# Causal attention of one stage: a hand-written order over both batches, the mask as a bf16 product, copies on ScalarE

## The chip, the cores and the metric

The kernel runs on one core of one Trainium2 chip. The time is device microseconds of one execution; lower is better. Three runs of the kernel before gave 4184.93, 4197.97 and 4197.70 us, with the median 4197.7 us. A fourth execution was profiled, and all durations below are from it.

## The reference

The kernel computes a network of eight layers on an input of 2 batches, 1024 positions and 128 features in fp32. Every layer is added to the running state `x`, after a normalisation of `x` over the features. The third layer, a causal attention with one head, is the one that the change touches:

```python
def _layernorm(x, axis=-1, eps=1e-05):
    m = jnp.mean(x, axis=axis, keepdims=True)
    v = jnp.var(x, axis=axis, keepdims=True)
    return (x - m) / jnp.sqrt(v + eps)

def _L0_attn_b_ref(x, wqk, wov):
    b, n, d = x.shape
    mask = jnp.triu(jnp.full((n, n), -jnp.inf, dtype=x.dtype), k=1)
    q = jnp.einsum('bnd,de->bne', x, wqk)
    scores = jnp.einsum('bne,bme->bnm', q, x) + mask
    attn = jax.nn.softmax(scores, axis=-1)
    ctx = jnp.einsum('bnm,bmd->bnd', attn, x)
    return jnp.einsum('bnd,de->bne', ctx, wov)
...
x = x + _L0_ffn_ref(_layernorm(x, axis=-1), ...)
x = x + _L0_attn_b_ref(_layernorm(x, axis=-1), L0_attn_b_wqk, L0_attn_b_wov)
x = x + _L0_ffn_ref(_layernorm(x, axis=-1), ...)
```

## The kernel before

The state lies in SBUF, features on the 128 partitions, in four tiles `xt[0]` to `xt[3]` of 512 positions; `xt[0]` and `xt[1]` are batch 0. The stages run one after another: the windowed attention `attn_a0`, the experts `ffn0`, the causal attention `attn_b0`, `ffn0` again, `attn_a1`, then the six deep layers (`Layers`) and the rest. In `attn_a0`, `ffn0` and `Layers` the order of the work on each engine is the order in which the program names it (`manual_schedule` with the engines of `ORDERED`). In `attn_b0` a scheduler puts the order together.

`attn_b0` (L237 to L290) first does, for each of the four blocks of 512 positions, a normalisation (`self.norm`): four transposes on TensorE (PE) at L120 so that positions lie on the partitions, statistics on VectorE (DVE; L124, L125), the inverse root on ScalarE (ACT; L134) and a reciprocal (L135), the scaling on DVE (L143), four transposes back (L152) and a copy to `xn` on ACT (L155). Then come the projection `pq` (L253) with its copy to `qT` on ACT (L254), and the product of the block with `wov`, `pw` (L257), with its copy to `xw` on DVE (L258). ACT reaches the square root and the exponential through different function tables, and a change of table is an instruction of its own in the profile (ACT_TABLE_LOAD).

The second loop goes over the batches and over eight blocks `i` of 128 query positions. For a block it computes the scores against all keys up to its own (L265; one or two products of up to 512 columns into a PSUM tile `sc`), adds the causal mask to the last 128 columns on DVE (L268), takes the negative maximum (L270), the exponential with its sum on ACT (L273) into `pr`, and the reciprocal of the sum (L274). Then the probabilities are transposed in groups of up to four blocks of keys (L163, called through `to_psum`), copied from PSUM to `pT` on DVE (L280) and multiplied with `xw` into `y` (L282). The result is divided by the sum on DVE (L286), transposed back (L288) and added to `xt` on DVE (L290). PSUM holds two banks for transposes and projections (tag `tp`), two score tiles of two banks each (`sc`) and one bank for `y`.

An fp32 product appears in the profile as two matmul instructions, a transpose as one.

Of the kernel before, what the change touches and what calls it, by code (L numbers as in the profile page):

```python
# [10 lines left out]
F32 = mybir.dt.float32  # L11
BF16 = mybir.dt.bfloat16
AF = mybir.ActivationFunctionType
ALU = mybir.AluOpType
AX = mybir.AxisListType
PSUM = bass.MemoryType.PSUM

P = 128
B, N, D = 2, 1024, 128
T = B * N  # L20
NBLK = T // 512
EPS = 1e-5
# [19 lines left out]
ORDERED = {  # L42
    mybir.EngineType.PE, mybir.EngineType.Activation, mybir.EngineType.DVE, mybir.EngineType.Pool,
}


class Net:
# [186 lines left out]

    def attn_b0(self, key):  # L237
        nc, tc = self.nc, self.tc
        with ExitStack() as ctx:
            cp = ctx.enter_context(tc.tile_pool(name="b0c", bufs=1))  # L240
            sb = ctx.enter_context(tc.tile_pool(name="b0s", bufs=2))
            ps = ctx.enter_context(tc.tile_pool(name="b0ps", bufs=2, space=PSUM))
            wqk, wov = self.w["b0"][:, 0:D], self.w["b0"][:, D : 2 * D]
            causal = self.w["b0_mask"]
            xn = [cp.tile([P, N], F32, tag=f"xn{b}", name=f"b0xn{b}") for b in range(B)]
            qT = [cp.tile([P, N], F32, tag=f"q{b}", name=f"b0q{b}") for b in range(B)]
            xw = [cp.tile([P, N // P, D], F32, tag=f"xw{b}", name=f"b0xw{b}") for b in range(B)]
            for b in range(B):
                for k in range(2):
                    x = xn[b][:, ts(k, 512)]  # L250
                    self.norm(self.xt[2 * b + k], x, ps, f"{key}_{b}_{k}")
                    pq = ps.tile([P, 512], F32, tag="tp", name=f"b0pq{b}{k}")
                    nc.tensor.matmul(pq, wqk, x, start=True, stop=True)  # L253
                    nc.scalar.copy(qT[b][:, ts(k, 512)], pq)  # L254
                    pw = ps.tile([P, 4, D], F32, tag="tp", name=f"b0pw{b}{k}")
                    for c in range(4):
                        nc.tensor.matmul(pw[:, c, :], x[:, ts(c, P)], wov, start=True, stop=True)  # L257
                    nc.vector.tensor_copy(xw[b][:, ts(k, 4), :], pw)  # L258
            for b in range(B):
                for i in range(N // P):  # L260
                    n = P * (i + 1)
                    sc = ps.tile([P, N], F32, tag="sc", name=f"b0sc{b}{i}")
                    for c in range(0, n, 512):
                        m = min(512, n - c)
                        nc.tensor.matmul(  # L265
                            sc[:, ds(c, m)], qT[b][:, ts(i, P)], xn[b][:, ds(c, m)], start=True, stop=True
                        )
                    nc.vector.tensor_tensor(sc[:, ts(i, P)], sc[:, ts(i, P)], causal, ALU.add)  # L268
                    mx = self.small.tile([P, 1], F32, tag="bmx", name=f"b0mx{b}{i}")
                    nc.vector.tensor_reduce(mx, sc[:, 0:n], AX.X, ALU.max, negate=True)  # L270
                    pr = sb.tile([P, N], F32, tag="pr", name=f"b0pr{b}{i}")
                    sm = self.small.tile([P, 1], F32, tag="bsm", name=f"b0sm{b}{i}")
                    nc.scalar.activation(pr[:, 0:n], sc[:, 0:n], AF.Exp, bias=mx, accum_out=sm)  # L273
                    nc.vector.reciprocal(sm, sm)  # L274
                    y = ps.tile([P, D], F32, tag="y", name=f"b0y{b}{i}", bufs=1)
                    for c in range(0, i + 1, 4):
                        m = min(4, i + 1 - c)
                        tp = self.to_psum(ps, "tp", lambda j: pr[:, ts(c + j, P)], f"b0tp{b}{i}{c}", m)
                        pT = sb.tile([P, 4, P], F32, tag="pT", name=f"b0pT{b}{i}{c}", bufs=3)
                        nc.vector.tensor_copy(pT[:, 0:m, :], tp[:, 0:m, :])  # L280
                        for j in range(m):
                            nc.tensor.matmul(  # L282
                                y, pT[:, j, :], xw[b][:, c + j, :], start=(c + j == 0), stop=(c + j == i)
                            )
                    o = sb.tile([P, D], F32, tag="o", name=f"b0o{b}{i}")
                    nc.vector.tensor_scalar(o, y, sm, None, ALU.mult)  # L286
                    tp = ps.tile([P, 4, P], F32, tag="tp", name=f"b0to{b}{i}")
                    nc.tensor.transpose(tp[:, 0, :], o, self.ident)  # L288
                    x = self.xt[2 * b + i // 4][:, ts(i % 4, P)]
                    nc.vector.tensor_tensor(x, tp[:, 0, :], x, ALU.add)  # L290

# [284 lines left out]
class Experts:  # L578
# [19 lines left out]
    def bank(self, tag, name):  # L598
        bufs = {"b": 4, "x3": 2, "h": 1, "x2": 1}[tag]
        return self.ps.tile([P, 512], F32, tag=tag, name=f"f0{name}_{self.key}", bufs=bufs)  # L600
# [863 lines left out]
```

## Time and profile before

| | |
|---|---|
| median of three runs | 4197.7 us (4184.93 to 4197.97) |
| profiled execution | 4190.64 us |
| its span, first to last instruction | 4188.8 us |
| mean granted clock of TensorE | 0.958 |
| PE, DVE, ACT, POOL busy, share of the span | 94%, 74%, 57%, 59% |
| `attn_b0`: first transposes (L120) to those of the next stage | 391.92 to 486.58 us |

The profile's page gives the busy time of each engine over the span, and cuts the span into 40 slices of 104.7 us in which each digit is a busy share in tenths. In its row PEclk the digit is the clock that TensorE was granted, in tenths of full speed. The busy time by stretch gives the same for any window. A timeline row has the start and the length in us, the engine, the line, the operation, the tiles written and read with their shapes, and in brackets how long the engine had been idle and whose work ended that. PEld are the weight loads of TensorE, which overlap its products. POOL is GpSimd.

### The profile page before, as it was taken

The numbers are of one execution on the slowest core, as the hardware profiler recorded it, in microseconds if no ns is written. First come the engines' busy times: TensorE is split into PE (matmuls) and PEld (weight loads), VectorE is DVE, ScalarE is ACT, GpSimd is POOL, SyncE is SP. The second block draws the span as 40 slices with busy tenths as digits, with TensorE's granted clock in tenths as the row PEclk, the third lists the DMA queues.
The fourth block names the chain that finished last, engine by engine and source line by source line (L and its number), as shares of the span: only waits on it lengthen the run. The fifth ranks groups of instructions, "written<-read, shape, count | busy, mean of one in ns | idle before, by whom it ended". The sixth has DMA issues, their size and how long they took to land.

```text
span 4188.8 us, 156424 instructions
## 1 busy us (share of the span) xinstructions
PE 3932.2 (94%) x67608; PEld 2556.2 (61%) x67608; DVE 3107.2 (74%) x5983; ACT 2401.4 (57%) x4507; POOL 2457.2 (59%) x1578
## 2 busy tenths in 40 slices
PE   7789796899999999999999848999999999999998
PEld 4543533566666666666666525666666666666665
DVE  6843545778878787878878657787887878787886
ACT  3433232676666666666666416766666666666665
POOL 1322022777677776776766217776766777667762
PEclk8789898999999999999999968999999999999999
DMA  1000001223233332232222103232233322323222
GB/s 56 2 1 1 1 0 32 81 71 84 74 76 84 76 85 72 73 90 71 69 66 68 45 16 91 73 84 74 74 84 76 84 73 72 91 68 77 62 67 56
DMA packets 181572, 261.53 MB, mean 62 GB/s; under 512 B 51100, under 2 KB 74264, under 8 KB 180632
## 3 DMA queue, kind: packets, MB, share of 16 engines
q1 hardware_dynamic: 180888, 251.52, 23.4%
q8 instruction: 538, 8.81, 0.9%
q14 instruction: 146, 1.20, 0.1%
HBM read 52.09 MB, written 1.05 MB: 13 GB/s over the span
## 4 chain that ended last, share of the span: by engine, by line
PE 82%; DVE 3%; ACT 1%; POOL 1%; issue 1%; DMA 0%; SPq 0%; ACTq 0%; DVEq 0%; POOLq 0%
PE pj_l L943 16%; PE y_l L1174 9%; PE pv_l L1045 9%; PE tqk_l L163 9%; PE av_l L1142 8%; PE sc_l L1092 6%; PE tpr_l L163 4%; PE to_l L163 4%; PE fg_l L1248 3%; PE fy_l L1284 3%; PE fa_l L1269 3%; PE sc_l L1083 2%; PE f0x_e L760 1%; PE f0h_e L693 1%; PE f0x_e L693 1%
## 5 line engine op out<-in xcount | busy, mean ns | idle before, releaser
L972 DVE TENSOR_TENSOR t_l<-pj_l,rot_l 128x512 f32<-128x512 f32 x1536 | 967.9, 684 | 370.3 <-ACT sq_l L952 357.4
L989 POOL TENSOR_TENSOR raw_l<-t_l,t_l 128x1024 f32<-128x1024 f32 x384 | 908.4, 2366 | 530.2 <-DVE on_l L1150 336.2
L943 PE MATMUL pj_l<-wqkv_l,x_l 128*128 128x512 f32 x1536 | 783.3, 612 | 8.1 <-DVE t_l L972 5.7
L1004 POOL TENSOR_TENSOR raw_l<-raw_l,rn_l 128x1024 f32<-128x1024 f32 x384 | 723.1, 1901 | 95.3 <-ACT rn_l L999 88.3
L952 ACT ACTIVATE sq_l<-pj_l 128x512 f32<-128x512 f32 x768 | 461.7, 603 | 369.4 <-PE pj_l L943 361.4
L978 POOL TENSOR_TENSOR sq_l<-sq_l 128x512 f32<-128x512 f32 x384 | 490.9, 1278 | 310.3 <-ACT sq_l L952 307.1
L163 PE MATMUL tqk_l<-ident_sb,raw_l 128*128 128x128 f32 x3072 | 453.2, 279 | 17.0 <-POOL raw_l L1004 14.7
L163 PEld LDWEIGHTS tqk_l<-ident_sb,raw_l 128*128 128x128 f32 x3072 | 356.9, 142 | 162.4 <-issue 123.4
L1022 ACT COPY qT_l<-tqk_l 128x512 f32<-128x512 f32 x384 | 224.8, 585 | 387.6 <-PE tqk_l L163 387.6
L1045 PE MATMUL pv_l<-wqkv_l,x_l 128*128 128x512 f32 x768 | 415.6, 623 | 5.8 <-DVE ln_xn_fl L1228 5.3
L1174 PE MATMUL y_l<-outT_l,wo_l 128*128 128x128 f32 x3072 | 393.7, 281 | 0.0
L1092 PEld LDWEIGHTS sc_l<-kT_l,qT_l 64*32 64x32 f32 x24576 | 294.9, 105 | 155.0 <-issue 144.4
L1174 PEld LDWEIGHTS y_l<-outT_l,wo_l 128*128 128x128 f32 x3072 | 357.5, 191 | 18.2 <-issue 1.0
L1142 PE MATMUL av_l<-vw_l,pT_l 64*32 64x64 f32 x24576 | 358.9, 224 | 3.7 <-issue 3.6
L943 PEld LDWEIGHTS pj_l<-wqkv_l,x_l 128*128 128x128 f32 x1536 | 255.0, 192 | 171.9 <-issue 106.6
L1054 ACT COPY v_l<-pv_l 128x512 f32<-128x512 f32 x384 | 225.0, 586 | 223.0 <-PE pv_l L1045 202.9
L1142 PEld LDWEIGHTS av_l<-vw_l,pT_l 64*32 64x32 f32 x24576 | 292.9, 105 | 71.9 <-issue 65.7
L1150 DVE TENSOR_TENSOR on_l<-av_l,inv_l 128x512 f32<-128x512 f32 x384 | 247.5, 686 | 120.0 <-PE av_l L1142 119.8
L1092 PE MATMUL sc_l<-kT_l,qT_l 64*32 64x64 f32 x24576 | 329.2, 223 | 0.0
L163 PEld LDWEIGHTS tpr_l<-ident_sb,pr_l 128*128 128x128 f32 x1536 | 188.9, 141 | 152.1 <-issue 116.2
L1102 DVE TENSOR_TENSOR pr_l<-sc_l,mx_l 128x512 f32<-128x512 f32 x384 | 265.6, 692 | 13.2
L1101 DVE TENSOR_REDUCE mx_l<-sc_l 128x8 f32<-128x512 f32 x384 | 261.4, 681 | 3.4 <-PE sc_l L1092 3.4
(344 smaller groups left out, 6158.1 us busy)
## 6 DMA issues: line engine op xcount, KB each, us to landing
vw_l<-v_l SPq DMA_DIRECT2D x3024, 64.0 KB
wqkv_l<-in_Wqkv SPq DMA_DIRECT2D x36, 512.0 KB
rot_l<-in_rotary SPq DMA_DIRECT2D x24, 512.0 KB
wo_l<-in_Wo SPq DMA_DIRECT2D x12, 512.0 KB
w_l<-in_W SPq DMA_DIRECT2D x12, 341.0 KB
f_sb<-in_f SPq DMA_DIRECT2D x1, 1936.0 KB
qks_l<-in_qk_scale SPq DMA_DIRECT2D x12, 128.0 KB
w_l<-in_W SPq DMA_DIRECT2D x12, 128.0 KB
```

Source lines behind the costliest of these rows:

```text
L163: self.nc.tensor.transpose(tp[:, c, :], src(c), self.ident)
L943: self.nc.tensor.matmul(pj.rearrange("p h d -> p (h d)"), self.x[b][0][:, ts(a, P)], self.w[i]["qkv"][:, ds(INNER * s + 512 * u, 512)], st ...
L952: self.nc.scalar.activation(st["sq", s][:, u], st["pj", s, u], AF.Square)
L972: self.nc.vector.tensor_tensor(to, st["pj", s, u], tabs[:, k, None, ts(w, LD // 2)].to_broadcast(half), ALU.mult)
L978: self.nc.gpsimd.tensor_tensor(sq[:, 0], sq[:, 0], sq[:, 1], ALU.add)
L989: self.nc.gpsimd.tensor_tensor(r.rearrange("p h u d -> p u h d"), st["t1", s], st["t2", s], ALU.add)
L1004: self.nc.gpsimd.tensor_tensor(r, r, st["rn"][:, ts(s, LH), None].to_broadcast([P, LH, LD]), ALU.mult)
L1045: self.nc.tensor.matmul(pj, self.x[b][0][:, ts(a, P)], self.w[i]["qkv"][:, ds(2 * INNER + 512 * r, 512)], start=True, stop=True,)
L1092: nc.tensor.matmul(sc[j][ts(c, 32), hp, :], st["q"][rows, hp, ts(c, 32)], st["k"][rows, hp, ds(32 * c, 64)], start=False, stop=(hp == 7),)
L1102: nc.vector.tensor_tensor(p, st["sc"][j], mx[:, :, None].to_broadcast([P, 8, 64]), ALU.subtract)
L1142: nc.tensor.matmul(av[r][ts(c, 32), q, j, :], st["pT", j][rows, q, ts(c, 32)], st["vw"][rows, c, ts(2 * q + j, LD)], start=True, stop=True,)
L1174: self.nc.tensor.matmul(y[:, 0:P], self.w[i]["o"][:, c, :], st["o"][:, c, :], start=(c == 0), stop=(c == 7))
```

## The change

The two loops of `attn_b0` are replaced by small functions, one for each part of the work, and a list of words that calls them. The stage then runs under `manual_schedule`, so that each engine does its parts in the order of the list. A word is a part with its place: `S13` is the scores of batch 1, block 3; `Tp041` the transposes of batch 0, block 4, second group of keys; `Tin2` the first transposes of `xt[2]`. The list mixes both batches and lets scores, exponentials, transposes and outputs of several blocks alternate.

Further edits: the mask is no longer added by DVE; after the scores TensorE adds it in PSUM as a product of a bf16 identity with a bf16 copy of the mask, both made once by DVE at the start of the stage. The copies of the transposed probabilities (`cp`) and of `xw` are done by ACT. The inverse root of the normalisation is an addition and a power on GpSimd (`rs`). The tag `tp` has three banks instead of two.

```diff
+B0_ORDER = """
+    Tin0 sta0 Tin1 rs0 sta1 rs1 x10 x11 Tx0 fx0 pq0 pw0 qT0 S00 Tx1 S02 mx00 ex00 S01 fx1 mx02 pq1
+    xw0 Tp000 pw1 ex02 mx01 qT1 ex01 cp000 S04 xw1 Tp010 Tp020 cp010 Tin2 Y000 mx04 S05 sta2 ex04
+    S03 on00 rs2 Y010 cp020 Tp040 mx05 ex05 Tp041 on01 x12 mx03 Y020 S06 To00 xa00 cp040 To01 cp041
+    ex03 Tp030 cp030 Tx2 on02 xa01 Tin3 sta3 Tp051 Y030 on03 S07 rs3 fx2 Y040 pq2 cp051 Y041 x13
+    To02 on04 Tx3 xa02 mx06 qT2 Tp050 fx3 pw2 To04 cp050 ex06 Y050 mx07 xa04 xw2 Tp061 Y051 cp061
+    To03 ex07 Tp060 xa03 on05 cp060 S13 To05 mx13 Tp071 Y060 ex13 cp071 S10 xa05 mx10 Y061 Tp130
+    on06 S11 mx11 cp130 To06 Tp070 cp070 ex10 ex11 xa06 pq3 qT3 Y070 Tp100 Tp110 Y071 S12 on07 S14
+    cp100 mx12 ex12 Y130 pw3 cp110 Tp120 mx14 on13 ex14 To07 Y100 xw3 cp120 S16 To13 xa07 on10 Y110
+    mx16 Tp141 S15 xa13 on11 To10 Tp140 ex16 S17 mx15 cp140 cp141 ex15 To11 xa10 Y120 xa11 Tp150
+    on12 Tp151 Y140 cp150 mx17 cp151 Y141 Tp161 on14 To12 xa12 cp161 Tp160 Y150 Y151 on15 ex17 To14
+    Tp170 cp160 xa14 Y160 Y161 cp170 To15 on16 xa15 Tp171 cp171 Y170 Y171 on17 To16 xa16 To17 xa17
+"""
...
-            causal = self.w["b0_mask"]
+            causal = cp.tile([P, P], BF16, tag="causal", name="b0causal")
+            nc.vector.tensor_copy(causal, self.w["b0_mask"])
+            identb = cp.tile([P, P], BF16, tag="identb", name="b0identb")
+            nc.vector.tensor_copy(identb, self.ident)
...
-            for b in range(B):
-                for k in range(2):
-                    x = xn[b][:, ts(k, 512)]
...
-                    nc.vector.tensor_tensor(x, tp[:, 0, :], x, ALU.add)
+            def bank(name, tag="tp", shape=(P, 4, P), bufs=3):
+                st[name] = ps.tile(list(shape), F32, tag=tag, name=f"b0{name}", bufs=bufs)
+                return st[name]
...
+            def sta(g):
+                s6, mv = small("ln_st", g, (P, 4, 6)), small("ln_mv", g, (P, 4, 2))
+                for c in range(4):
+                    nc.vector.bn_stats(s6[:, c, :], st[f"in{g}"][:, c, :])
+                    nc.vector.bn_aggr(mv[:, c, :], s6[:, c, :])
+
+            def rs(g):
+                r = small("ln_rs", g, (P, 4))
+                nc.gpsimd.tensor_scalar_add(r, st["ln_mv", g][:, :, 1], EPS)
+                nc.gpsimd.tensor_tensor(r, r, self.nhalf, ALU.pow)
...
+            def put_xw(g):
+                nc.scalar.copy(xw[int(g) // 2][:, ts(int(g) % 2, 4), :], st[f"pw{g}"])
+
+            def S(b, i):
+                i = int(i)
+                n = P * (i + 1)
+                sc = bank(f"sc{b}{i}", "sc", (P, N), 2)
+                q, x = qT[int(b)][:, ts(i, P)], xn[int(b)]
+                for c in range(0, n, 512):
+                    m = min(512, n - c)
+                    last = c + m == n
+                    nc.tensor.matmul(sc[:, ds(c, m)], q, x[:, ds(c, m)], start=True, stop=not last)
+                    if last:
+                        nc.tensor.matmul(sc[:, ts(i, P)], identb, causal, start=False, stop=True)
...
+            def Tp(b, i, c):
+                tp = bank(f"tp{b}{i}{c}")
+                for j in range(keys(i, c)):
+                    nc.tensor.transpose(tp[:, j, :], st["pr", b + i][:, ts(4 * int(c) + j, P)], self.ident)
+
+            def cp_(b, i, c):
+                m = keys(i, c)
+                nc.scalar.copy(tl("pT", b + i + c, (P, 4, P), 3)[:, 0:m, :], st[f"tp{b}{i}{c}"][:, 0:m, :])
...
+            def on(b, i):
+                sm = st["bsm", b + i]
+                nc.vector.reciprocal(sm, sm)
+                nc.vector.tensor_scalar(tl("o", b + i, (P, D)), st[f"y{b}{i}"], sm, None, ALU.mult)
...
+            with tc.manual_schedule(engines=ORDERED):
+                for word in B0_ORDER.split():
+                    name = word.rstrip("0123456789") if not word.startswith("x1") else "x1"
+                    parts[name](*word[len(name):])
```

The parts that are not shown do what the lines before did: `Tin` L120, `x1` L143, `Tx` L152, `fx` L155, `pq` L253, `qT` L254, `pw` L257, `mx` L270, `ex` L273, `Y` L282, `To` L288 and `xa` L290. `on` is L274 and L286 together.

More of the change, by code (lines that the diff above doesn't have):

```diff
@@ L247, in attn_b0 @@
             xw = [cp.tile([P, N // P, D], F32, tag=f"xw{b}", name=f"b0xw{b}") for b in range(B)]
-            for b in range(B):
-                for k in range(2):
-                    x = xn[b][:, ts(k, 512)]
[L251 to L290, printed above, removed]
@@ new lines, in attn_b0, with tl, small @@
+            st = {}
+            def bank(name, tag="tp", shape=(P, 4, P), bufs=3):
+                st[name] = ps.tile(list(shape), F32, tag=tag, name=f"b0{name}", bufs=bufs)
+                return st[name]
+            def tl(tag, k, shape, bufs=2):
+                st[tag, k] = sb.tile(list(shape), F32, tag=tag, name=f"b0{tag}{k}", bufs=bufs)
+                return st[tag, k]
+            def small(tag, k, shape):
+                st[tag, k] = self.small.tile(list(shape), F32, tag=tag, name=f"b0{tag}{k}")
+                return st[tag, k]
@@ new lines, in of_block, with flat, Tin @@
+            def of_block(x, g):
+                return x[int(g) // 2][:, ts(int(g) % 2, 512)]
+            def flat(x):
+                return x.rearrange("p c d -> p (c d)")
+            def Tin(g):
+                tp = bank(f"in{g}")
+                for c in range(4):
+                    nc.tensor.transpose(tp[:, c, :], self.xt[int(g)][:, ts(c, P)], self.ident)
+            def sta(g):
+                s6, mv = small("ln_st", g, (P, 4, 6)), small("ln_mv", g, (P, 4, 2))
+                for c in range(4):
+                    nc.vector.bn_stats(s6[:, c, :], st[f"in{g}"][:, c, :])
+                    nc.vector.bn_aggr(mv[:, c, :], s6[:, c, :])
@@ new lines, in rs, with x1 @@
+            def rs(g):
+                r = small("ln_rs", g, (P, 4))
+                nc.gpsimd.tensor_scalar_add(r, st["ln_mv", g][:, :, 1], EPS)
+                nc.gpsimd.tensor_tensor(r, r, self.nhalf, ALU.pow)
+            def x1(g):
+                x, mv, r = tl("x1", g, (P, 4, P)), st["ln_mv", g], st["ln_rs", g]
+                for c in range(4):
+                    nc.vector.tensor_scalar(
+                        x[:, c, :], st[f"in{g}"][:, c, :], mv[:, c, 0:1], r[:, c : c + 1],
+                        ALU.subtract, ALU.mult,
+                    )
@@ new lines, in Tx, with pq, pw @@
+            def Tx(g):
+                tp = bank(f"tx{g}")
+                for c in range(4):
+                    nc.tensor.transpose(tp[:, c, :], st["x1", g][:, c, :], self.ident)
+            def pq(g):
+                nc.tensor.matmul(
+                    bank(f"pq{g}", shape=(P, 512)), wqk, of_block(xn, g), start=True, stop=True
+                )
+            def pw(g):
+                p, x = bank(f"pw{g}"), of_block(xn, g)
+                for c in range(4):
+                    nc.tensor.matmul(p[:, c, :], x[:, ts(c, P)], wov, start=True, stop=True)
@@ new lines, in mx, with ex @@
+            def mx(b, i):
+                n = P * (int(i) + 1)
+                nc.vector.tensor_reduce(
+                    small("bmx", b + i, (P, 1)), st[f"sc{b}{i}"][:, 0:n], AX.X, ALU.max, negate=True
+                )
+            def ex(b, i):
+                n = P * (int(i) + 1)
+                nc.scalar.activation(
+                    tl("pr", b + i, (P, N))[:, 0:n], st[f"sc{b}{i}"][:, 0:n], AF.Exp,
+                    bias=st["bmx", b + i], accum_out=small("bsm", b + i, (P, 1)),
+                )
@@ new lines, in keys, with Y @@
+            def keys(i, c):
+                return min(4, int(i) + 1 - 4 * int(c))
+            def Tp(b, i, c):
[5 more added lines that the diff above has]
+                nc.scalar.copy(tl("pT", b + i + c, (P, 4, P), 3)[:, 0:m, :], st[f"tp{b}{i}{c}"][:, 0:m, :])
+            def Y(b, i, c):
+                if c == "0":
+                    bank(f"y{b}{i}", "y", (P, D), 1)
+                for j in range(keys(i, c)):
+                    k = 4 * int(c) + j
+                    nc.tensor.matmul(
+                        st[f"y{b}{i}"], st["pT", b + i + c][:, j, :], xw[int(b)][:, k, :],
+                        start=(k == 0), stop=(k == int(i)),
+                    )
@@ new lines, in on, with To, xa @@
+            def on(b, i):
+                sm = st["bsm", b + i]
+                nc.vector.reciprocal(sm, sm)
+                nc.vector.tensor_scalar(tl("o", b + i, (P, D)), st[f"y{b}{i}"], sm, None, ALU.mult)
+            def To(b, i):
+                nc.tensor.transpose(bank(f"to{b}{i}")[:, 0, :], st["o", b + i], self.ident)
+            def xa(b, i):
+                x = self.xt[2 * int(b) + int(i) // 4][:, ts(int(i) % 4, P)]
+                nc.vector.tensor_tensor(x, st[f"to{b}{i}"][:, 0, :], x, ALU.add)
@@ new lines, in attn_b0 @@
+            parts = {
+                "Tin": Tin, "sta": sta, "rs": rs, "x1": x1, "Tx": Tx,
+                "fx": lambda g: nc.scalar.copy(of_block(xn, g), flat(st[f"tx{g}"])), "pq": pq,
+                "qT": lambda g: nc.scalar.copy(of_block(qT, g), st[f"pq{g}"]), "pw": pw, "xw": put_xw,
+                "S": S, "mx": mx, "ex": ex, "Tp": Tp, "cp": cp_, "Y": Y, "on": on, "To": To, "xa": xa,
+            }
+            with tc.manual_schedule(engines=ORDERED):
+                for word in B0_ORDER.split():
+                    name = word.rstrip("0123456789") if not word.startswith("x1") else "x1"
+                    parts[name](*word[len(name):])
```

## The prediction

> **What bounds the kernel now.** First the slices of the whole span: TensorE is busy almost everywhere, but around the fifth slice (each is 104.7 us) DVE, ACT and PE have a hole, and the granted clock dips.
>
> ```profile
> PE   7789796899999999999999848999999999999998
> PEclk8789898999999999999999968999999999999999
> ```
>
> The timeline places the changed stage there: its first transposes start at 391.92 us, the next stage's at 486.58 us. So at most 94.66 us, 2.3% of the span, can change. Then the busy time of each engine by stretch (columns: length, PE, weight loads, DVE, ACT, POOL, granted clock, DMA share, GB/s): the whole stage, its first 36 us, its last 39 us, and for comparison two stages whose order was also written by hand, the experts (270 to 390) and the windowed attention (80 to 210).
>
> ```profile
> 391.92:486.58 94.66, 72.61 (x352) 49.17 (x353) 52.33 (x160) 22.91 (x47) 1.26 (x1) 0.87 0.00 1
> 392.00:428.00 36.00, 24.75 (x81) 15.28 (x81) 16.39 (x66) 10.80 (x20) 1.26 (x1) 0.74 0.00 0
> 448.00:487.00 39.00, 32.46 (x202) 23.83 (x203) 23.83 (x63) 7.76 (x18) 0.00 (x0) 1.00 0.00 1
> 270.00:390.00 120.00, 119.03 (x346) 45.00 (x345) 45.87 (x68) 43.01 (x69) 38.09 (x31) 1.00 0.00 1
> 80.00:210.00 130.00, 104.16 (x1947) 76.59 (x1949) 109.10 (x144) 64.36 (x97) 50.05 (x27) 0.70 0.01 2
> ```
>
> In the stage PE is idle 94.66 - 72.61 = 22.1 us, and part of its busy time is slow: the clock is 0.74 in the first 36 us. The timeline of the last query block shows what the idle time is:
>
> ```profile
> 481.99 1.20 PE L163 MATMUL b0tp<-ident_sb,b0pr 128*128 128x128 f32 x8
> 482.62 1.30 DVE L280 COPY b0pT<-b0tp 128x512 f32<-128x512 f32 x2
> 483.37 2.05 PE L282 MATMUL b0y<-b0xw,b0pT 128*128 128x128 f32 x16 [0.18 <-DVE b0pT L280]
> 485.46 0.35 DVE L286 TENSOR_SCALAR b0o<-b0y,b0sm 128x128 f32<-128x128 f32 x1 [1.54 <-PE b0y L282]
> 485.87 0.33 PE L288 MATMUL b0to<-ident_sb,b0o 128*128 128x128 f32 x1 [0.45 <-DVE b0o L286]
> 486.23 0.29 DVE L290 TENSOR_TENSOR xt<-b0to,xt 128x128 f32<-128x128 f32 x1 [0.42 <-PE b0to L288]
> ```
>
> One block goes round PE, DVE, PE, DVE, PE, DVE, and PE has nothing of another block to do. The bound is this chain of single blocks, and ahead of it (392 to 428) four normalisations one after another; no engine is full.
>
> **The change, part by part.** The start of each engine's list is as the word list has it: both Tin, two blocks of statistics, Tx0, pq0, pw0, and scores of batch 0 before batch 1 is normalised. From there I price PE's work at full clock and ask what keeps PE from it.
>
> *Head.* The first transposes stay at 391.92. DVE now first makes the two bf16 copies, and the first of them may only start when POOL's last addition of the stage before (row L768, 392.00 + 1.26) has given its memory free: 393.3. Two copies at 0.28 (nearest row: L280 with 128x128): 393.9. Then the statistics of two blocks, eight pairs: the next stage's eight take 487.27 to 490.50, 3.23 us: 397.1. GpSimd's root (0.23 + 1.03, rows L131 and L132 there) runs under the second block's four. From the start of the scaling (L143) to the copy of the transposed block it was 394.43 to 396.44, 2.0 us, and 0.64 to the projection behind the copy: pq0 starts at 399.7 instead of 397.08. Head: 7.8 us.
>
> *PE's work behind the head, at full clock.* Distances inside warm groups: 16 passes of 128 columns in 2.05 less the last one's 0.27, over 15, are 0.119; four transposes take 0.60 (L163), (0.60 - 0.27)/3 = 0.11; two passes of 512 take 1.02 (L265), so 1.02 - 0.59 = 0.43. Four projections of two passes of 512: 3.4. Sixteen value products of two passes: 3.8. Remaining transposes of the normalisation, 20: 2.2. Scores, 2 x 36 tiles of 128 columns in two passes, 18,432 columns: 15.5. Transposed probabilities 72: 7.9. Outputs 144 passes: 17.1. Transposes back 16: 1.8. Sum 51.7, the same work as before.
>
> *Mask.* Removed from DVE: 16 additions of 0.295 (L268), 4.7 us, which stood between scores and maximum. Added to PE: 16 bf16 products of 128x128 with a weight load. No row of that shape exists. Lower bound 0.09, one bf16 weight load of L1083 (mean 89 ns, in the later layers); upper bound 0.24, two fp32 passes. An addition to PE can't be a gain. I take 0.12, one pass of 128 columns as the rows above have it: 1.9 us (1.4 to 3.8). [...]
>
> *Copies to ScalarE.* 24 copies L280 (12.6 us) and 4 of L258 (2.8) leave DVE. On ACT a 128x512 copy takes 0.585 (L254); narrow ones have no row, so each lies between 0.27 (0.585 less 384 columns at 0.83 ns, the slope of L273's rows, 367 ns at 128 to 1114 at 1024) and 0.585. ACT then has 8 copies (4.7), 4 of xw (2.3), 24 of probabilities (11.4, at most 14.0), exponentials 11.8 with 3.1 for their sums, one table load 1.3: 35 us. DVE: statistics 6.5, scaling 5.5, maxima 11.9, reciprocals 2.6, L286 5.6, L290 4.6, two copies 0.6: 37 us. Both lie beside 54 us of PE and I cost them at nothing. Without that cover a late copy holds the Y behind it and all that is queued on PE; with three instead of two transposing banks there is one more block of slack.
>
> *Removed beside the path.* Three table loads (1.28 each: 390.45, 403.47, 410.35 and 426.51 become one), four roots on ACT, four reciprocals (0.18). The one load left lies behind qT0 while PE does pw0 and S00: nothing.
>
> *Clock.* The stage before: 0.50 in 396 to 400, back to 1.00 at 402.5, then down again at 405.9, after a stretch in which PE was busy 59% (402 to 406, 2.37 of 4.00). In the new order PE has no such hole once pq0 has started, so I take one slow stretch: pq0 and pw0, 1.8 us of work, at half clock cost 1.8 more, and 0.7 for what follows: 2.5 us (1 to 12).
>
> *Gaps.* PE's idle share is 1% in the experts' ordered stage and 6.54/39 = 17% in the last stretch here. The order mixes several blocks like the experts', with more kinds of waits: 5%, 2.8 us (0.5 to 11).
>
> *Tail.* Behind the last Y: 0.17 + 0.35 + 0.33 + 0.29 with 0.04 at each change of engine: 1.2.
>
> Sum: 7.8 + 51.7 + 1.9 + 2.5 + 2.8 + 1.2 = 67.9 against 94.66: 26.8 us less. Nothing behind the stage changes: SP's list is the same row for row, and so are the other engines' outside the stage. The next stage's first transposes wait for DVE's last xt, as before. The profiled execution took 4190.64 us (span 4188.8, 1.8 around it): 4163.9. The three runs shown have the median 4197.7, 7 us above it, and one at 4184.93; from the median the same gain gives 4170.9. I forecast the middle, **4167 us**.
>
> **Rivals.**
> *Gaps as in the other ordered stage.* A fixed order stalls all behind one late word. In 80 to 210 PE is idle (130 - 104.16)/130 = 20%, though DVE is the full engine there, which it won't be here. Then (51.7 + 1.9 + 2.5)/0.8 + 9.0 = 79.1: 15.5 less, 4175 to 4182 with the two bases.
>
> *The clock keeps dropping.* Short holes between the groups keep the clock at the 0.74 of 392 to 428: 53.6/0.74 + 2.8 + 9.0 = 84.2, 10.4 less: within the bound, near 4184. For it: the ordered stage at 80 to 210 has 0.70 with PE 80% busy. Against: those are small tiles, and this stage has 1.00 from 448 on with PE 83% busy. [...]
>
> *Slower: the clock never comes back.* At a clock c the stage lasts 53.6/c + 11.8; it passes 94.66 from c = 0.647 downwards. At 0.55, near the half clock of 424 to 432 with PE busy 85%, it is 109.3: 14.6 more, 4205 to 4212. For it: 80 to 90 shows 0.58 with PE 87% busy. Against: 1.00 from 434 onwards.
>
> *The saving isn't there*, because the list doesn't overlap what its words say, a copy or tile waiting for a whole batch. For it: one xn and one qT tile serve both blocks of a batch. Against: the present kernel already reads one half while the other is written (scores at 401.5, second half copied at 406.6). Then about the present time, 4191 to 4198.
>
> **How the numbers follow.** Forecast 0.74 (stage 64 to 74 from the middle base, and 5 either way for that base: 4158 to 4179), gaps 0.13, clock dropping 0.08, slower 0.03, no saving 0.02. A measurement of this kernel tells about 0.3% (12.6 us) from no change. Forecast and gaps are faster by more: 0.87; dropping clock and no saving lie within: 0.10; slower 0.03. Low end: PE 53.1 with the cheap mask, gaps 0.5, clock 1, so 63.6, 31 less than the lowest run: 4153. High end: the median less the dropping clock's gain: 4187.
>
> **What would show it.** In the profile after: the stage 64 to 74 us long; PE idle under 6 us behind pq0; pq0 starting 2 to 3 us later than before; granted clock 1.00 from about 12 us into the stage; DVE and ACT 35 to 40 us each; one table load; mask products at 0.1 to 0.2 each. Wrong would be: PE waiting for ACT's copies, a clock below 0.9 in the stage's second half, or a time above 4187.

## The result and the profile after

The changed kernel takes 4161.6 us (median of 5, 4155.37 to 4168.74), the kernel before 4185.58 (median of 5: the three runs known ahead and two more, 4181.71 to 4197.97). The ratio is 0.9933, with a 95% interval from 0.9911 to 0.9955: 19 to 37 us less. The profiled execution of the changed kernel took 4168.74 us, with a span of 4167.0, and is the longest of its five.

The first view is the page's row of slices for the changed kernel (tenths of busy time, then of granted clock). The hole around the fifth slice is gone from PE's row (7 before, 9 now); the clock's digit there stays 8, since the slice also holds the start of the next stage, where the clock falls (458.95 us):

```profile
PE   7889995999999999999999848999999999999998
PEclk8689897999999999999999868999999999999999
```

The stage now runs from 392.97 us (first transposes, now L292) to 456.96 us (first transposes of the next stage, L136). Busy time by stretch of the changed kernel, with the columns of before (length, PE, weight loads, DVE, ACT, POOL, granted clock, DMA share, GB/s): the whole stage, the part behind the first projection pq0, and 52 us in its middle.

```profile
392.97:456.96 63.99, 58.18 (x369) 44.63 (x369) 33.76 (x114) 30.75 (x69) 6.30 (x9) 0.95 0.00 1
400.45:456.96 56.51, 55.66 (x357) 43.04 (x357) 28.14 (x89) 30.16 (x68) 2.52 (x4) 0.97 0.00 1
404.00:456.00 52.00, 51.77 (x347) 40.38 (x345) 27.15 (x86) 28.74 (x67) 2.52 (x4) 1.00 0.00 1
```

The stage lost 94.66 - 63.99 = 30.7 us. PE's idle time fell from 22.1 to 5.8 us, which is 16.2 us of it, and PE's busy time from 72.61 to 58.18, which is 14.4 us, although 16 products were added. Only a part of these 14.4 us is the clock. PE's busy time times the missing share of the clock, summed over windows of 0.5 us, gives 10.6 us lost before and 2.7 us after. So about 8 us, a quarter of the gain, is the same work at a higher clock. The other 6.5 us are, by my estimate, the ends of groups: a product that stands last in its group or alone is shown with its full length (0.27 us for 128 columns), while products that follow closely stand 0.119 us apart.

What PE waited for in the stage, first before the change, then after it (total us, times, longest):

```profile
PE ln_out_e L152 <- DVE ln_xn_e L143: 8.9, 4, 2.6
PE b0y L282 <- DVE b0pT L280: 3.9, 10, 0.8
PE b0to L288 <- DVE b0o L286: 3.5, 7, 0.9
PE b0sc L265 <- ACT b0pr L273: 3.0, 3, 1.2
PE b0pq L253 <- ACT b0xn L155: 2.1, 3, 0.8
PE ln_in_e L120 <- DVE f0x_e L767: 0.9, 1, 0.9
```

```profile
PE b0tx L316 <- DVE b0x L308: 4.2, 1, 4.2
PE b0in L292 <- DVE f0x_e L876: 0.9, 1, 0.9
PE b0pq L319 <- ACT b0xn L392: 0.7, 1, 0.7
PE ln_in_e L136 <- DVE xt L388: 0.4, 1, 0.4
PE b0to L384 <- DVE b0o L381: 0.3, 1, 0.3
```

Before, five kinds of wait came back 27 times (the sixth row is the wait for the stage ahead). After, each row is one single wait: three lie ahead of pq0, one belongs to the next stage, and the only one inside is the tail's 0.3 us. No copy of probabilities and no exponential is among PE's waits any more.

The timeline of the changed kernel shows why. Between the exponential of one block and its transposes, PE does the scores, the mask and the transposes of others:

```profile
427.14 0.60 PE L362 MATMUL b0tp<-ident_sb,b0pr 128*128 128x128 f32 x4
427.16 1.12 ACT L351 ACTIVATE b0pr<-b0sc,b0bmx 128x1024 f32<-128x1024 f32 x1
...
427.57 1.02 PE L339 MATMUL b0sc<-b0xn,b0q 128*128 128x512 f32 x2
...
428.01 0.10 PEld L341 LDWEIGHTS <-b0identb 128*128 128x128 bf16 x1 [0.24 <-issue]
...
428.44 0.22 PE L341 MATMUL b0sc<-b0causal,b0identb 128*128 128x128 bf16 x1
...
428.49 0.28 PE L384 MATMUL b0to<-ident_sb,b0o 128*128 128x128 f32 x1
```

The mask product of 428.44 is shown as 0.22 us long, but the next product starts 0.05 us behind it: what it occupies is the distance, not the length.

Of the two profiled executions the changed one is only 21.9 us shorter, 8.8 us less than the stage gave. Does something behind the stage give time back? The time outside the stage (the run's time less the stage's length) is 4096.0 us in the profile before and 4104.8 after. In the twelve profiles below, whose stages last from 61.0 to 186.9 us, it lies between 4090.7 and 4101.9 with no relation to the stage. So it scatters by some 14 us from run to run, and the profile after is the highest of all fourteen. For this reason the stage's length in the trace is the measure of each experiment, not the whole time.

The stage's length has a scatter of its own, and each experiment is one profiled execution. The one version that was profiled twice gave 61.00 and 61.01 us, but its clock stays at 1.00. In the change the clock is 0.50 for 3.88 us from pq0 on. In three experiments whose head is as long, 7.5 us (copies on DVE, five mask products, each copy twice) it is 0.50 for only 3.11 us, and with the mask on DVE for 4.53 us. The last section has the likely reason: the clock's changes lie 3.41 us or a multiple of it apart. Half of such a difference goes into the stage, so I read nothing from differences below 0.7 us between two single profiles.

### The profile page after: what moved, and what is told of

The parts are those of the page before. It is cut to its first block, busy times and chain, and to the rows that moved or that the text cites. A ratio compares the mean times of both kernels' runs of the same rounds, so it can differ in the third digit from the quotient of the medians.

```text
span 4167.0 us, 156464 instructions
## 1 busy us (share of the span) xinstructions
PE 3926.2 (94%) x67624; PEld 2556.5 (61%) x67624; DVE 3087.2 (74%) x5937; ACT 2409.2 (58%) x4528; POOL 2462.6 (59%) x1586
## 4 chain that ended last, share of the span: by engine, by line
PE 89%; DVE 6%; ACT 2%; issue 1%; POOL 1%; DMA 1%; SPq 0%; DVEq 0%; ACTq 0%; POOLq 0%
PE pj_l L1052 16%; PE y_l L1283 9%; PE pv_l L1154 9%; PE tqk_l L179 9%; PE av_l L1251 8%; PE sc_l L1201 7%; PE tpr_l L179 4%; PE to_l L179 4%; PE fy_l L1393 3%; PE fg_l L1357 3%; PE fa_l L1378 3%; PE sc_l L1192 2%; PE f0x_e L869 1%; PE f0h_e L802 1%; PE f0x_e L802 1%
```

## The experiments

The theory: PE's work bounds the stage once the list puts other blocks' work into each wait; so the order is the gain, and the other edits count only where they keep that order fed. The rivals: the work taken off DVE is the gain; or ScalarE, the clock or waits set what is left.

**The parts without the order.** The words go block by block, as the old loops did, and the list is not fixed:

```diff
+    Tin0 sta0 rs0 x10 Tx0 fx0 pq0 qT0 pw0 xw0 Tin1 sta1 rs1 x11 Tx1 fx1 pq1 qT1 pw1 xw1 Tin2 sta2 rs2
+    x12 Tx2 fx2 pq2 qT2 pw2 xw2 Tin3 sta3 rs3 x13 Tx3 fx3 pq3 qT3 pw3 xw3 S00 mx00 ex00 Tp000 cp000 Y000
+    on00 To00 xa00 S01 mx01 ex01 Tp010 cp010 Y010 on01 To01 xa01 S02 mx02 ex02 Tp020 cp020 Y020 on02
...
-            with tc.manual_schedule(engines=ORDERED):
-                for word in B0_ORDER.split():
...
+            for word in B0_ORDER.split():
```

> Every part of the change is in (mask product, copies on ScalarE, the root on GpSimd, three banks for transposed probabilities), but the words stand block by block as in the old loops, and the engines' order is left to the planner. Theory (the order is what counts: PE's work bounds the stage once blocks overlap): the parts alone shorten the single-block chain only a little, stage 80 to 92 us against 94.66 before and 63.99 with the change. Rival (taking 20 us of work off DVE, and three table loads off ScalarE, is what counts): stage below 70 us without any hand-written order.

Measured: stage 94.31 us, 0.35 less than before the change (whole time 4186.38). Busy time of the stage, and below it what PE waited for:

```profile
387.52:481.83 94.31, 72.50 (x368) 50.61 (x368) 33.61 (x114) 30.78 (x69) 6.29 (x9) 0.86 0.00 1
```

```profile
PE b0tx L316 <- DVE b0x L308: 13.7, 4, 4.2
PE b0y L373 <- ACT b0pT L366: 3.6, 9, 0.6
PE b0pq L319 <- ACT b0xn L392: 2.1, 3, 0.7
PE b0to L384 <- DVE b0o L381: 1.7, 4, 0.4
```

DVE lost 18.7 us of work and PE gained nothing: its idle time is 21.8 us, as it was. The four normalisations stand one after another again, and are longer (13.7 us in four waits, 8.9 before), mostly by the root, which takes GpSimd about 1.3 us where ScalarE and DVE took 0.5. By these lists that eats what the shorter block chain saves, about 4 us: the waits add up to 21.4 us before and 21.1 here. The rival is out, and the 80 to 92 us that I gave the theory were still too hopeful: taken together, the parts alone are worth nothing. What mask and copies would give without the slower root was not run.

**A fixed order, but block by block.** The change as it is, only with that list of words.

> The change with its fixed order, but the list itself goes block by block: every engine meets S, maximum, exponential, transposes, copies, Y, and the way back of one block before the next block's. Theory (what counts is that the list puts another block's work on PE in each wait): PE stands through some 3 to 4 us of waits in each of 16 blocks and through four heads of about 5 us, stage 110 to 130 us, longer than before the change. Rival (a fixed order of any kind, or the moved work, is what counts): stage below 75 us.

Measured: stage 186.90 us (390.85 to 577.75), whole time 4280.35. The waits of PE and the busy time:

```profile
PE b0tp L362 <- ACT b0pr L351: 29.1, 16, 2.6
PE b0tx L316 <- DVE b0x L308: 15.9, 4, 4.6
PE b0y L373 <- ACT b0pT L366: 14.5, 24, 0.7
PE b0to L384 <- DVE b0o L381: 7.1, 16, 0.4
```

```profile
390.85:577.75 186.90, 117.14 (x369) 75.03 (x369) 37.05 (x114) 33.09 (x69) 6.29 (x9) 0.59 0.00 0
```

PE is idle for 69.8 us, which is what 16 blocks and four heads make and what I had expected. What I had not: beside these holes the clock is 0.59 over the whole stage, and the same products take 117 us instead of the 58 with the change. Of the 117, 54 us are lost to the clock, summed as above, against 2.7 with the change. A fixed order is no gain in itself; what its list interleaves is. My 110 to 130 us had the work at full clock.

**The mask on DVE.** The bf16 product and its two copies are left out, and `mx` adds the mask first:

```diff
-                    if last:
-                        nc.tensor.matmul(sc[:, ts(i, P)], identb, causal, start=False, stop=True)
...
+                sc = st[f"sc{b}{i}"][:, ts(int(i), P)]
+                nc.vector.tensor_tensor(sc, sc, causal, ALU.add)
```

> The change, but the mask is added by DVE again (16 additions of about 0.3 us, 4.7 us in all), the bf16 products and the two bf16 copies are left out. Theory (DVE has room beside PE: 34 us of work in 64): PE loses 0.9 us of products, the head loses 0.5 us of copies, the additions lie beside other blocks' PE work: stage 62 to 66 us. Rival (the additions between scores and maximum hold PE, as they did in the block chain): 64 + 4.7 - 1.4 = 67 us or more.

Measured: 64.11 us, 0.12 more than the change. The head is 6.51 us instead of 7.48, the part behind pq0 57.60 instead of 56.51. So no gain of the mask product can be seen here. Leaving out its two copies saves 0.97 us in the head, and the part behind it is 1.09 longer, of which some 0.3 is the longer half clock (4.53 us against 3.88).

**The copies on DVE.** `cp` and `xw` use `nc.vector.tensor_copy` instead of `nc.scalar.copy`.

> The change, but the copies of transposed probabilities and of xw are made by DVE again (about 14 us of work moved from ScalarE to DVE). Theory: DVE then has 48 of 64 us, still less than PE; but its list holds them in an order written for another engine, so a few are late: stage 64 to 69 us. Rival (DVE's load is what bound the stage, so the move to ScalarE is what the gain is): the stage grows by about the work given back, 74 to 80 us.

Measured: 68.41 us, 4.4 more than the change. PE now waits for DVE's copies; three rows of its waits:

```profile
PE b0tp L362 <- DVE b0pT L366: 0.8, 2, 0.4
...
PE b0y L373 <- DVE b0pT L366: 0.7, 2, 0.5
PE b0pq L319 <- DVE b0pT L366: 0.7, 1, 0.7
```

13.7 us of work went back to DVE, and a third of that showed up. So the move to ScalarE has its place in the fixed order, though DVE is busy for only 47 of 68 us here and not full: the copies are late in its list.

**The root on ScalarE.** The change with the root and the reciprocal of before, which brings the table loads back:

```diff
-                nc.gpsimd.tensor_scalar_add(r, st["ln_mv", g][:, :, 1], EPS)
-                nc.gpsimd.tensor_tensor(r, r, self.nhalf, ALU.pow)
+                nc.scalar.activation(r, st["ln_mv", g][:, :, 1], AF.Sqrt, bias=self.eps)
+                nc.vector.reciprocal(r, r)
```

> The change, but the root of the normalisation is taken by ScalarE with a reciprocal on DVE, as before the change, so that ScalarE loads its tables anew between exponentials and roots (1.28 us each). Theory (the loads stand in front of exponentials that the fixed order already waits for; the hole they make on PE also brings back the half clock): most of the 8 to 12 us by which the order alone was longer: stage 70 to 76 us, clock at 0.50 for some microseconds behind 414. Rival (the loads lie beside PE's work, and it was the load on DVE): stage 64 to 67 us.

Measured: 68.31 us, 4.3 more, between the two expectations. The head is 8.60 us instead of 7.48, because DVE's reciprocals now stand in its list and wait for the roots. Behind pq0 the timeline shows one of the table loads:

```profile
427.09 1.28 ACT L351 ACT_TABLE_LOAD   x1
...
428.39 1.01 ACT L351 ACTIVATE b0pr<-b0sc,b0bmx 128x896 f32<-128x896 f32 x1
...
429.54 0.55 PE L362 MATMUL b0tp<-ident_sb,b0pr 128*128 128x128 f32 x3 [1.19 <-ACT b0pr L351]
```

The exponential is late by the load, and PE stands 1.19 us, nearly the whole load. But the hole is short, and the clock stays at 1.00 from 410 us on: the dip that the theory gave behind 414 us did not come. Of the 4.3 us, 2.9 are idle time of PE and 1.4 longer busy time with a clock of 0.50 until 406.75 us, which is 6.16 us from pq0 on instead of 3.88. The exponential starts 0.02 us behind the load, and the load 0.02 us behind the copy ahead of it (a row of 426.49 us, 0.58 long), so what the trace shows of a switch is the load's 1.28 us alone.

**The order without the parts.** The fixed order, with mask and copies on DVE and the root on ScalarE (the three edits above in one; three `tp` banks stay).

> The fixed order alone: mask added by DVE, copies made by DVE, root and table loads on ScalarE with a reciprocal on DVE, as before the change (the three banks for transposed probabilities stay, since the list needs them). Theory (the order alone makes the gain; the parts alone gave 94.31 us): the 68.4 us of the run with DVE's copies, with 4.7 us of additions and three or four table loads of 1.28 us more beside PE: stage 68 to 76 us. Rival (order and parts need each other, since DVE now has over 50 us in a list written for less): stage above 80 us.

Measured: 76.32 us, 0.3 above what the theory gave and 18.3 less than before the change. The three parts undone one by one cost 0.1, 4.4 and 4.3; together they cost 12.3. Where the other 3.5 may come from can be read from three stretches of 4 us (columns as above):

```profile
414.00:418.00 4.00, 1.68 (x13) 1.09 (x10) 3.83 (x11) 2.27 (x3) 0.00 (x0) 0.91 0.00 0
418.00:422.00 4.00, 3.62 (x6) 1.45 (x6) 0.71 (x3) 2.06 (x3) 0.00 (x0) 0.50 0.00 0
422.00:426.00 4.00, 3.79 (x16) 3.19 (x17) 2.30 (x8) 0.00 (x0) 0.00 (x0) 0.50 0.00 0
```

and from the timeline at their start:

```profile
412.13 1.28 ACT L299 ACT_TABLE_LOAD   x1
...
413.43 0.30 ACT L299 ACTIVATE b0ln_rs<-b0ln_mv,eps 128x4 f32<-128x4 f32 x1
...
413.76 0.18 DVE L300 RECIPROCAL b0ln_rs<-b0ln_rs 128x4 f32<-128x4 f32 x1 [0.52 <-ACT b0ln_rs L299]
...
415.65 1.28 ACT L348 ACT_TABLE_LOAD   x1 [1.93 <-DVE b0bsm L377]
...
416.16 0.94 PE L370 MATMUL b0y<-b0xw,b0pT 128*128 128x128 f32 x6 [1.33 <-DVE b0o L378]
...
417.99 3.35 PE L336 MATMUL b0sc<-b0xn,b0q 128*128 128x512 f32 x4 [0.90 <-ACT b0pr L348]
```

A load on ScalarE delays a root, and the reciprocal behind it stands at the head of DVE's list for 0.52 us with copy, mask and maximum queued behind. DVE is then busy for 3.83 of 4 us, PE waits 1.33 us for a division at the end of that queue and 0.90 us for an exponential that a second load delays, and it is busy for only 1.68 of 4 us. Then the clock is 0.50: in 418 to 426 PE is busy for 7.4 us at half speed, which alone loses 3.7 us. That this is the missing 3.5 us is read from one trace; no run separates it from the rest. The third `tp` bank is in this run too, so its share of the 18.3 us is not known.

**Five mask products instead of one.**

```diff
-                        nc.tensor.matmul(sc[:, ts(i, P)], identb, causal, start=False, stop=True)
+                        for r in range(5):
+                            nc.tensor.matmul(sc[:, ts(i, P)], identb, causal, start=False, stop=(r == 4))
```

> The change with each mask product issued five times (64 more; so the mask counts five times, and masked scores stay far below the others). Theory (PE's work is the bound, and one product takes 0.05 us there): 64 x 0.05 = 3.2 us more, stage 66.5 to 68 us. Rival (what is left is set by waits, not by PE's work): stage unchanged, 63.5 to 65 us. By the predicted 0.12 us a product it would be 71.7 us.

Measured: 66.87 us. 2.88 us for 64 products is 0.045 us each; the half clock behind pq0 is 0.77 us shorter here than in the change, which is worth about 0.4 us, so 0.05 us is nearer. That is the distance in the timeline above. PE's work goes through to the end at full price, so PE is the bound behind pq0.

**Each probability copy twice.**

```diff
-                nc.scalar.copy(tl("pT", b + i + c, (P, 4, P), 3)[:, 0:m, :], st[f"tp{b}{i}{c}"][:, 0:m, :])
+                pT = tl("pT", b + i + c, (P, 4, P), 3)
+                for r in range(2):
+                    nc.scalar.copy(pT[:, 0:m, :], st[f"tp{b}{i}{c}"][:, 0:m, :])
```

> The change with each copy of transposed probabilities made twice by ScalarE (24 more, 11.5 us; ScalarE's work from 31 to 42 of 64 us). Theory (the copies lie beside PE's work): a few are late, stage 64 to 68 us. Rival (ScalarE's copies are on the path between transposes and Y, and each holds PE): 24 x 0.48 us more, stage 73 to 76 us.

Measured: 68.06 us, 0.06 above what the theory gave. Of 10.7 us of work added to ScalarE, 4.1 reach the end. As with the copies on DVE, a later copy is partly covered, not wholly.

**Products in the head.** The first projections run at a clock of 0.50 (until 404.33 us in the change) behind a hole of PE of 4.22 us. Nine products whose result is not used fill that hole:

```diff
+            def hot(n):
+                w = bank("hot", "sc", (P, N), 2)
+                for r in range(int(n)):
+                    nc.tensor.matmul(w[:, 0:512], self.ident, self.xt[0], start=True, stop=True)
...
+    Tin0 sta0 Tin1 hot9 rs0 sta1 rs1 x10 x11 Tx0 fx0 pq0 pw0 qT0 S00 Tx1 S02 mx00 ex00 S01 fx1 mx02 pq1
```

> The change with nine products of 128x512 (fp32, 0.43 us apart, result unused) on PE behind the second block's first transposes, in the time in which PE waits for the statistics, about 4 us. Theory (the half clock of the first projections comes from PE's hole ahead of them): the clock stays up, pq0 and pw0 take 1.8 us less: stage 61.5 to 63 us. Rival (the clock falls because of what went before, or comes back at a fixed time): stage 63.5 to 65 us, clock at 0.50 behind pq0 as without them.

Measured: 64.98 us. Busy time behind pq0:

```profile
402.72:457.71 54.99, 54.05 (x357) 41.76 (x357) 27.86 (x88) 30.04 (x68) 2.52 (x4) 1.00 0.00 1
```

The length is in the rival's range, but the rival is wrong: the clock is 1.00 in every stretch of 4 us from 390 to 446, and behind pq0 the stage takes 54.99 us instead of 56.51. I had mis-sized the filling: an fp32 product is two passes of 0.43 us, nine of them took 7.89 us instead of 4, and pq0 came at 9.99 us instead of 7.48.

**Another head.** `bf` makes the two bf16 copies, `sta` does four statistics and then four means, and block 0 is scaled first:

```diff
-    Tin0 sta0 Tin1 rs0 sta1 rs1 x10 x11 Tx0 fx0 pq0 pw0 qT0 S00 Tx1 S02 mx00 ex00 S01 fx1 mx02 pq1
+    Tin0 sta0 Tin1 rs0 bf x10 Tx0 sta1 rs1 fx0 pq0 pw0 qT0 S00 x11 Tx1 S02 mx00 ex00 S01 fx1 mx02 pq1
```

> The change with another head: the two bf16 copies under GpSimd's root, block 0 scaled and transposed before block 1's statistics, four statistics before their four means. Theory (the head is a chain on DVE of which PE waits for each link): 1.4 us for POOL and the copies and some 2 us of statistics off it, of which GpSimd's root gives back 0.9: pq0 5.5 to 6 us behind the first transposes (7.48 now), stage 62 to 63 us. Rival (the second block is then late by as much): stage 63.5 to 65 us.

Measured: 62.79 us, pq0 5.97 us behind the first transposes. 1.5 us came off the head, and the part behind pq0 is 0.3 longer; the half clock lasts 4.97 us from pq0 on here, 3.88 in the change.

**That head with four products** (`hot4` behind `Tin1`).

> The same head, with four products of 128x512 (fp32, two passes of 0.43 us each, result unused) on PE behind the second block's first transposes, 3.4 us in all, so that they end about when Tx0 can start. Theory (half clock behind pq0 comes from the hole ahead of it; behind pq0 the run with nine products took 54.99 us against 56.51): head 5.5 to 6.2, stage 60.5 to 61.5 us, clock 1.00 throughout. Rival (the hole that is left between Tx0 and pq0, or the second block's late statistics, brings the half clock back): stage 62 to 64 us.

Measured: 61.00 us. Busy time of the stage and of the part behind pq0, then the head in the timeline:

```profile
392.75:453.75 61.00, 59.03 (x376) 44.55 (x377) 32.17 (x114) 30.90 (x69) 6.32 (x9) 1.00 0.00 1
398.58:453.75 55.17, 53.93 (x356) 41.76 (x357) 28.31 (x92) 30.32 (x68) 3.76 (x6) 1.00 0.00 1
```

```profile
393.68 3.60 PE L320 MATMUL b0hot<-xt,ident_sb 128*128 128x512 f32 x8
...
396.10 1.37 DVE L312 TENSOR_SCALAR b0x<-b0in,b0ln_mv,b0ln_rs 128x128 f32<-128x128 f32 x4 [1.24 <-POOL b0ln_rs L307]
...
397.11 0.74 PE L325 MATMUL b0tx<-ident_sb,b0x 128*128 128x128 f32 x4
...
398.58 1.13 PE L328 MATMUL b0pq<-b0xn,b_sb 128*128 128x512 f32 x2 [0.73 <-ACT b0xn L401]
```

The clock is 1.00 throughout; against the same head without the products, the part behind pq0 is 1.65 us shorter. The two projections at half clock were worth that.

**That kernel, timed.** The same kernel in four runs, and the kernel before in seven.

> The kernel with the new head and the four products, timed against the kernel before. Theory: the stage of 61.0 us against 94.66 carries over whole, 33.7 us, 3 us more than the change alone: ratio near 0.992, stage again 60.5 to 61.5 us in its trace. Rival (something behind the stage gives the gain back, as the change's own profile looked, where 30.7 us in the stage were 21.9 us over all): ratio 0.994 to 0.996.

Measured: 4154.74 us (median of 4, 4147.62 to 4157.41), the kernel before beside it 4191.73 (median of 7, 4183.74 to 4201.21): ratio 0.9905, interval 0.9883 to 0.9926, stage 61.01 us. The gain of 31 to 49 us holds the stage's 33.7, and nothing behind the stage gives it back. This version beats both: the kernel before by this ratio, and the change by its stage. Its interval overlaps that of the change (0.9911 to 0.9955), so the second rests on the stage's 61.00 and 61.01 us against 63.99, not on the whole times.

## Why the prediction was right

4167 us was predicted and 4161.6 measured; the stage 67.9 us, and 63.99 measured, a hundredth below the 64 to 74 that were named as a sign. By its steps:

- *The bound, a chain of single blocks.* Right. The parts without the order leave the stage at 94.31 us; the order without the parts takes 18.3 us off.
- *Head, 7.8 us.* 7.48 us, by the steps as given: the casts waited for POOL's last addition until 394.36 us, and the root lay under the second block's statistics.
- *PE's work 51.7 and tail 1.2, together 52.9.* What is left of the 56.51 us behind pq0 when clock (1.5), mask (0.7) and idle time (0.85) are taken off is 53.4, by difference, with the tail's idle time counted in the 0.85. The run with nine products in the head confirms it: at a clock of 1.00 PE is busy for 54.05 us behind pq0, 53.3 without the mask.
- *Mask, 1.9.* Mis-sized: five products for one give 0.045 to 0.05 us a product, 0.7 to 0.8 in all. I had priced it as a pass of 128 fp32 columns (0.12), with 0.09, a weight load, as the lower bound. Both are too high: the load takes PE no time of its own, since it lies under the scores ahead of it (L341's weight load at 428.01 us, its product at 428.44).
- *Clock, 2.5.* One slow stretch at pq0 and pw0, as predicted; it cost 1.5 us by the products in the head. That is less than the 1.8 for the projections alone, so the 0.7 for what follows does not show.
- *Gaps, 2.8 (5%).* The largest error: 0.85 us, 1.5%, with the tail's in it. The bound between 1% (experts) and 17% was right, and the list is as tight as the experts'.
- *Copies at nothing.* Right here: no wait of PE for a probability copy is left. How far the cover reaches is now measured: of 10.7 us more copying on ScalarE 4.1 us reach the end, of 13.7 us on DVE 4.4.
- *Table loads beside the path, nothing.* Right for the sum, but not as a reading of what the edit is worth: in the fixed order the root on ScalarE costs 4.3 us. That the loads lay beside the path of the old loops was read from their trace; no run takes them alone out of the kernel before.
- *DVE and ACT 35 to 40 us each.* 33.76 and 30.75: sums of mean lengths are too high, since neighbours on an engine overlap by about 0.1 us (the exponential of 427.16 us runs 1.12, the next row starts at 428.17). In the trace after, too, the lengths of all rows add up to 37.5 us on DVE and 35.0 on ACT.

The mechanism was right and these sizes were off: head, mask, clock and gaps add to -0.3 - 1.2 - 1.0 - 1.9 = -4.4, the work gives back 0.5, and -3.9 is the difference of the stage. That the whole time came out within 5.4 us is in part luck. The forecast started from 4194 us, the middle of 4190.64 and 4197.7; with two more runs the kernel before has the median 4185.58, and its five runs lie up to 16 us apart. The two medians differ by 24.0 us, less than the stage's 30.7, and the interval of 19 to 37 us holds both. Of the rivals, gaps of 20% were 1.5%, and the clock behind pq0 was 0.97, not 0.74. The slower rival, a low clock over the whole stage, is real: the list in block order has it, at 0.59 for 187 us. There PE waits for each of the 16 exponentials, and in this list for none. That the saving isn't there was excluded by the trace: no tile waits for a whole batch.

## What to carry to other kernels

Where one chain goes round several engines, moving its work to another engine need not shorten the stage as long as only one chain runs (here 18.7 us off DVE gave 0.35 us, with a root that became slower); first interleave independent chains, then move the work that is late in the new order. A fixed order is only as good as its list: the same code took 64 or 187 us. When PE's holes close, count the clock too: about a quarter of this gain, 8 of 30.7 us, was PE's own work at a higher clock.

## What was not expected of the hardware

- The clock is 0.50 or 1.00 in and around this stage, and its changes lie on a grid of 3.41 us in each of the eleven profiles that show more than one change (before: 395.66, 402.49, 405.91, 409.32, 416.14, 419.56, 422.97 and 433.21 us). In the stage before, it fell behind the steps of that grid in which PE was busy for 1.09, 1.78, 1.86 and 1.06 of 3.41 us (32, 52, 55 and 31%), but not behind two with 1.73 and 1.80 us (51 and 53%; they end at 412.73 and 446.87 us). It came back behind steps with 3.35 to 3.41 us (98 to 100%) and stayed at 0.50 behind steps with 2.20 to 2.74 us (65 to 80%). A little behind the stage it fell behind a step with 2.12 us (62%, 501.48 to 504.89 us), and stayed at 0.50 behind the next one, in which PE was busy throughout. So I read no limit from these shares.
- The clock also halved without a long hole. In the run with the order alone the step from 413.87 to 417.29 us has PE busy for 1.81 of 3.42 us (53%), with 1.33 us as the longest wait; the clock was then 0.50 until 427.53 us, though PE was busy for 8.94 of these 10.24 us.
- Four products, 3.60 us of PE, whose result nobody uses, put into a hole that can't be closed, made the work behind them 1.65 us shorter, and the head did not grow (5.83 us with them, 5.97 without).
- A bf16 product of 128x128 costs PE 0.045 to 0.05 us here, weight load included. That was measured with four more behind the first; the first, behind an fp32 group, stands 0.05 us ahead of the next product.
- Outside the changed stage the same program takes 4090.7 to 4104.8 us from run to run, nearly five times the 3 us between the change and the best version.
